# Four layers of long convolutions and a Haar mixing on one core: where the inverse transform's columns, the sums into z and the level steps run

## The chip, the core and the metric

The kernel runs on one core of a Trainium2 chip. A core has a matrix engine (TensorE, in the profile PE, with its weight loads as PEld), VectorE (DVE), ScalarE (ACT), GpSimd (POOL) and SyncE (SP), which here only issues transfers. PE writes its results into PSUM; DVE and ACT read PSUM and the on-chip memory SBUF; GpSimd reads and writes SBUF alone. Each engine works through its own instructions in order and waits for other engines by semaphores. The metric is the device time of one execution in microseconds (us), as the median over runs.

## The reference

The input x has 4 batches of 64 channels of 256 x 256 fp32 values. Four layers follow each other. Layers 0, 1 and 3 are convolutions whose filter is an outer product of two one-dimensional filters, plus a bias term; layer 2 is a two-dimensional Haar transform, a mixing of the channels with a soft threshold, the inverse transform and a residual sum.

```python
# layers 0, 1, 3
hx = _implicit_filter(z, Xw1, Xb1, Xw2, Xb2, Xw3, Xb3, Xwo, Xfreq, t, deltas)
hy = _implicit_filter(z, Yw1, Yb1, Yw2, Yb2, Yw3, Yb3, Ywo, Yfreq, t, deltas)
k = jnp.einsum('ijk,imk->ijmk', hx, hy)[0]
...
y = jnp.fft.irfft2(u_f * k_f, s=(fft_size, fft_size))[..., :L, :L]
out = y + x * bias[:, None, None]

# layer 2
f1 = haar2d(x)
for i in range(v.shape[0]):          # two paths
    f3 = f1 * v[i]
    f4 = jnp.einsum('bchw,oc->bohw', f3, conv_w[i])
    f5 = jnp.sign(f4) * jax.nn.relu(jnp.abs(f4) - tau[i])
    acc = acc + f5
y = haar2d(acc, inverse=True)
return y + x
```

## The kernel before, in words

A separable convolution of one channel is two products with triangular Toeplitz matrices (`contract`, L257 to L262): `first` makes pa, which ACT copies to a (L275), and `second` makes py, to which DVE adds the input times the bias (L292). That DVE step reads py from PSUM and one operand from SBUF. For layer 0 its result is called y0, for layer 1 y1, for layer 3 y3. `pairs` (L337, L338) begins the forward Haar transform along the row on DVE, `levels` goes on with it: lengths 128 and 64 on DVE, the five smaller ones in ten small steps on GpSimd for four channels at a time (L350, L351). `split`, `rest` and `down` turn the columns by two PE matmuls with an fp32r matrix of signs (pz, L381), and `away` sends the coefficients to memory.

`mixing` then takes the coefficients in 64 groups g a batch. `mix` multiplies with the channel weights into a PSUM tile px (L449); `scaled` on DVE (L468) and `scaled_too` on ACT (L473, one instruction of 64 columns each) multiply by v and leave f4. Of 16 parts of a group, N_ACT go to ACT. `size` (ACT, L477) writes the magnitude into the tile mag, of which there are two buffers; `sign` (ACT, L480) follows in place; `shrink` (DVE, L484) takes tau off, `signed` (DVE, L488) clamps at zero and multiplies by the sign, both with two SBUF operands; `add` (L494) sums the two paths into two rows of z, in two steps of 256 columns. The next size on the same mag buffer, two groups later, waits for that add. z holds a whole batch: four chunks of 16 channels.

`inverse` takes the 64 channels of z out. `fetch` (ACT, L534) copies one channel, `rows` (L541, L542) transposes and transforms along one axis on PE into a PSUM tile pw. The other axis is done in two ways. For chunk 0 (c < 16), `halves` splits pw into two fp32r parts (an ACT cast L548 and a DVE subtraction L549) and `cols` multiplies each with a matrix of signs on PE into pu (L555). For chunks 1 to 3 the transform is done ahead in z by DVE: `level` runs `halve` (a subtraction L299 and a scalar_tensor_tensor L300) for n = 1, 2, 4 up to 64 row pairs. The largest levels are cut into pieces of 16 row pairs, 1024 columns. `join` (L563, then L566 and L567) adds the kept residual r to pw or pu and interleaves the result into u. Then layer 3 follows, except for every third channel of batches 0 to 2, which `aside` stores and `convolution` takes up again during mixing 3, in place of the next batch's convolutions.

The order of the work: each stage is put into a list of events by `at`, with a time in ticks from the table PLACE; the list is sorted and recorded in that order. A scheduler then orders each engine's instructions by this order and by what is ready, so a step whose inputs are ready can be moved ahead of others. `tc.add_manual_dep` draws an edge between two instructions that keeps their order on the engine without a semaphore. While mixing b runs, batch b + 1 goes through layers 0 and 1 (`spread`), and inverse b follows the mixing.

Of the kernel before, what the change touches and what calls it, by code (L numbers as in the profile page):

```python
# [12 lines left out]
ALU = mybir.AluOpType  # L13
# [3 lines left out]
B, C, S, EMB, ORD = 4, 64, 256, 33, 64  # L17
# [3 lines left out]
GT = 4  # L21
BUFS = {"res": 1, "y": 5, "co": 3}

N_ACT = (12, 12, 12, 8)

PLACE = {
    "load": 0.714,
    "a0": 1.643,
    "a0 copy": 1.643,
    "y0": 2.571,  # L30
    "y0 sum": 2.571,
    "a1": 3.5,
    "a1 copy": 3.5,
    "y1": 4.429,
# [63 lines left out]
def conv_seq_kernel(ctx, tc, x, fz, fw, bias, decay, haar, haar_row, factors, vt, taut, wmix, out):  # L98
# [14 lines left out]
    nc = tc.nc  # L113
# [19 lines left out]
    bsb = const.tile([P, 3, C], F32, name="bsb")  # L133


    z = zpool.tile([P, 4, P, 4, 16], F32, name="z")
# [118 lines left out]
    def bank(name):  # L255
        return psm.tile([P, 2, S], F32, name=name, tag="mm")

    def contract(ps, src, t):

        for m in range(2):  # L260
            nc.tensor.matmul(ps[:, m, :], src[:, 0, m * P : (m + 1) * P], t[:, ::-1], start=True, stop=False)  # L261
            nc.tensor.matmul(ps[:, m, P:], src[:, 1, m * P : (m + 1) * P], t[:, : P - 1 : -1], start=False, stop=True)  # L262
# [16 lines left out]
    def second(b, st, key, layer, res, new, tag, ahead=None):  # L279


        def product(c):
            s = st[c]
            if ahead is not None:
                s[ahead] = toeplitz(ahead, c, f"t{ahead}_{b}_{c}")
            s["p" + new] = bank(f"p{new}_{b}_{c}")
            contract(s["p" + new], s[key], s[layer][:, 1, :])

        def residual(c):
            s = st[c]  # L290
            y = io.tile([P, 2, S], F32, name=f"{new}_{b}_{c}", tag=tag, bufs=BUFS[tag])
            nc.vector.scalar_tensor_tensor(y, s[res], bsb[:, layer, c : c + 1], s["p" + new], ALU.mult, ALU.add)  # L292
            s[new] = y

        return [product, residual]

    def halve(even, odd):

        nc.vector.tensor_sub(odd, even, odd)  # L299
        nc.vector.scalar_tensor_tensor(even, even, 2.0, odd, ALU.mult, ALU.subtract)  # L300

    def level(n, chunk, begin=0, count=None):
# [3 lines left out]
        halve(v[:, begin : begin + count, 0, 0, :], v[:, begin : begin + count, 1, 0, :])  # L306

    def butterfly():

# [9 lines left out]
    def at(time, run, unit):  # L319
        events.append((time, len(events), run, unit))  # L320
# [104 lines left out]
    def mixing(b, start, n_act):  # L425

        st = {}

        def load(g):
            f = mx.tile([P, 2, S], F32, name=f"f_{b}_{g}", tag="f", bufs=3)  # L430
            nc.sync.dma_start(f, coef[b].rearrange("k c p w -> (k c) p w")[:, 2 * g : 2 * g + 2])
            st[g] = {"f": f}
            if g % GT == 0:
                t = mx.tile([P, 2, GT, 16], F32, name=f"vt_{b}_{g}", tag="vt")
                nc.sync.dma_start(t, scales[g // GT])
                st["vt", g // GT] = t

        def scale(g, i):
            return st["vt", g // GT][:, i, g % GT, :]

        def over(g, i, n):
            return scale(g, i)[:, :n].unsqueeze(2).to_broadcast([P, n, C])

        def mix(g):
            f = st[g]["f"]
            ps = psx.tile([P, 2, 2, S], F32, name=f"px_{b}_{g}", tag="mix")
            for q in range(2):
                for h in range(2):
                    nc.tensor.matmul(  # L449
                        ps[:, q, h, :],  # L450
                        f[:, q, h * P : (h + 1) * P],
                        wb.rearrange("p r n -> p (r n)"),
                        start=True,
                        stop=True,
                    )
            if g == 0:

                one, two = ps[:, 0, :, :P], ps[:, 0, :, P:]
                d = mx.tile([P, 2, P], F32, name=f"d_{b}", tag="mag")
                nc.vector.tensor_copy(d, two)  # L460
                nc.vector.tensor_sub(two, one, d)
                nc.vector.tensor_add(one, one, d)
            st[g]["f4"] = mx.tile([P, 16, C], F32, name=f"f4_{b}_{g}", tag="f4")
            st[g]["px"] = ps.rearrange("p q h (r i o) -> p (q h r i) o", r=2, i=2)

        def scaled(g):
            px, n = st[g]["px"], 16 - n_act
            nc.vector.tensor_tensor(st[g]["f4"][:, :n], px[:, :n], over(g, 0, n), ALU.mult)  # L468

        def scaled_too(g, half):  # L470
            px, f4 = st[g]["px"], st[g]["f4"]
            for j in range(16 - n_act + half * (n_act // 2), 16 - (1 - half) * (n_act - n_act // 2)):
                nc.scalar.mul(f4[:, j], px[:, j], scale(g, 0)[:, j : j + 1])  # L473
# [12 lines left out]
        def signed(g):  # L486
            mag = st[g]["mag"]
            nc.vector.scalar_tensor_tensor(mag, mag, 0.0, st[g]["f4"], ALU.max, ALU.mult)  # L488

        def add(g):  # L490
            parts = st.pop(g)["mag"].rearrange("p (q x i) (n c) -> p q i x n c", q=2, i=2, n=4)
            for q in range(2):
                to = slot(2 * g + q)
                nc.vector.tensor_add(  # L494
                    z[:, :, to].rearrange("p n x c -> p x n c"), parts[:, q, 0], parts[:, q, 1]
                )


        for g in range(S // 4):
            for name, stage in zip(  # L500
                ("mix load", "mix", "scaled", "scaled too", "scaled rest", "size", "sign", "shrink", "signed", "add"),
                (
                    load,
                    mix,
                    scaled,
                    lambda g: scaled_too(g, 0),
                    lambda g: scaled_too(g, 1),
                    size,
                    sign,
                    shrink,  # L510
                    signed,
                    add,
                ),
            ):
                at(start + g + PLACE[name if b + 1 < B else "l " + name], stage, g)

    def inverse(b, start, put_off):

        st = {}

        def early(c):
            tag, bufs = ("f", 3) if c < 20 or c % 5 < 3 else ("f4", 2)
            r = mx.tile([P, 2, 2, P], F32, name=f"r_{b}_{c}", tag=tag, bufs=bufs)
            nc.sync.dma_start(r, keep[b][c])
            st[c]["r"] = r
# [34 lines left out]
        def join(c):  # L560
            ps = st[c]["pw"]
            t = io.tile([P, 2, 2, P], F32, name=f"t_{b}_{c}", tag="res", bufs=BUFS["res"])
            nc.vector.scalar_tensor_tensor(t, st[c]["r"], 0.5, ps, ALU.mult, ALU.add)  # L563
            u = io.tile([P, 2, S], F32, name=f"u_{b}_{c}", tag="y", bufs=BUFS["y"])
            v = u.rearrange("p m (w e) -> p m w e", e=2)
            nc.vector.tensor_add(v[:, :, :, 0], t[:, 0], t[:, 1])  # L566
            nc.vector.tensor_sub(v[:, :, :, 1], t[:, 0], t[:, 1])  # L567
            st[c]["u"] = u
# [3 lines left out]

        along = start - groups - 3

        def when(tick, n, chunk, *span):
            at(tick + PLACE["level"], lambda _: level(n, chunk, *span), 0)
# [88 lines left out]
    ahead = C  # L665
# [128 lines left out]
```

## Time and profile before

| what | us |
|---|---|
| median of 3 runs (2875.58 to 2878.57) | 2876.38 |
| the profiled execution | 2874.07 |
| its span in the trace | 2872.3 |
| ACT: a copies L275, 768 | 478.8 |
| ACT: scaled parts L473, 2816 | 610.5 |
| DVE: shrink L484 and signed L488, 256 each | 316.6 each |
| DVE: residual sums y0 and y1, L292, 256 each | 190.9 and 190.7 |
| DVE: levels of 1024 columns, L299 and L300, 84 each | 102.6 and 103.0 |
| POOL: all | 334.4 |

The profile shows each engine's busy time, and, for a group of instructions, the count, the summed time, the mean of one in ns, and the idle time of the engine ahead of it with what ended that idle time. Times in the trace count from the start of the span. The records of neighbouring instructions on an engine overlap a little, since an instruction is recorded from its start to its last write, so a sum of records can be larger than the time that the engine gave to them.

The batches' mixings lie, by the px matmuls, at 455 to 854, 1072 to 1507, 1720 to 2156 and 2366 to 2637 us; one group takes 6.28, 6.89, 6.89 and 4.31 us in them. The inverses, by the zc copies, lie at 868 to 1062, 1522 to 1711, 2171 to 2361 and 2650 to 2868.

### The profile page before, as it was taken

Reading aid. Unit: us, or ns where it says so; the run is one execution under the profiler, and the core shown is the slowest. Engines: PE = TensorE matmul, PEld = TensorE weight load, DVE = VectorE, ACT = ScalarE, POOL = GpSimd, SP = SyncE. Lnnn points to the kernel's source line nnn. Section 1 sums busy time; section 2 is a strip of 40 time slices with the busy share of each in tenths; the row PEclk is TensorE's granted clock in tenths of the full one; section 3 lists DMA queues with packets and bytes.
Section 4 is the critical chain, followed back from the end, with each engine's and each line's share of the span. In section 5 each row is a group of like instructions: output and inputs, shape, how many; then the busy total and the mean of one; then the engine's idle time right before and its main releaser. Section 6 shows DMA issues by size and latency. Waiting matters only on the chain. (4 is left out here: it accounts for less than half of the span.)

```text
span 2872.3 us, 52434 instructions
## 1 busy us (share of the span) xinstructions
PE 2827.1 (98%) x16592; PEld 2555.6 (89%) x16592; DVE 2494.9 (87%) x4255; ACT 2080.3 (72%) x4950; POOL 334.4 (12%) x644
## 2 busy tenths in 40 slices
PE   9999999999999999999999999999999999999999
PEld 7899998898888898998898998998898998888998
DVE  4655558999999779999999779999999779999985
ACT  2333338999995558998985658999995659998554
POOL 0111111121121001221221001121121000000000
PEclk9999999999999999999999999999999999999999
DMA  6878787776667986777777986777777988787786
GB/s 182 249 231 230 232 232 227 207 208 204 205 209 213 289 254 198 214 213 214 209 207 236 299 255 196 213 214 216 208 208 235 297 266 235 229 238 212 224 241 201
DMA packets 599367, 649.77 MB, mean 226 GB/s; under 512 B 48465, under 2 KB 517044, under 8 KB 598964
## 3 DMA queue, kind: packets, MB, share of 16 engines
q1 hardware_dynamic: 536996, 578.61, 68.9%
q10 hardware_dynamic: 62096, 67.82, 6.7%
q8 instruction: 134, 2.20, 0.3%
q14 instruction: 141, 1.16, 0.1%
HBM read 426.77 MB, written 219.48 MB: 225 GB/s over the span
## 5 line engine op out<-in xcount | busy, mean ns | idle before, releaser
L261 PE MATMUL py<-t,a 128*128 128x256 f32 x3072 | 922.5, 382 | 9.5 <-ACT a L275 8.7
L275 ACT COPY a<-pa 128x512 f32<-128x512 f32 x768 | 478.8, 623 | 498.6 <-PE pa L262 455.2
L473 ACT ACTIVATE f<-px,vt 128x64 f32<-128x64 f32 x2816 | 610.5, 367 | 101.6 <-DVE f L468 101.1
L262 PEld LDWEIGHTS py<-t,a 128*128 128x128 f32 x3072 | 583.4, 190 | 79.3
L262 PE MATMUL py<-t,a 128*128 128x128 f32 x3072 | 590.0, 274 | 0.0
L261 PEld LDWEIGHTS py<-t,a 128*128 128x128 f32 x3072 | 497.3, 191 | 51.2 <-ACT a L275 19.0
L449 PE MATMUL px<-wb,f 128*128 128x256 f32 x2048 | 487.6, 380 | 7.6 <-ACT f L473 7.6
L449 PEld LDWEIGHTS px<-wb,f 128*128 128x128 f32 x2048 | 369.0, 190 | 50.0 <-ACT f L473 10.5
L351 POOL TENSOR_TENSOR sd<-less 128x128 f32<-128x128 f32 (+4 forms) x320 | 190.8, 596 | 1858.7 <-DVE less L350 1519.9
L534 ACT COPY zc<-z 128x512 f32<-128x512 f32 x256 | 282.1, 1105 | 108.1 <-PE pw L542 99.0
L484 DVE TENSOR_TENSOR mag<-mag,vt 128x1024 f32<-128x1024 f32 x256 | 316.6, 1237 | 12.3 <-ACT mag L477 11.5
L488 DVE SCALAR_TENSOR_TENSOR mag<-mag,f 128x1024 f32<-128x1024 f32 x256 | 316.6, 1238 | 0.0
L261 PE MATMUL pa<-t,y 128*128 128x256 f32 x1024 | 309.1, 384 | 6.8 <-DVE y L292 5.2
L261 PE MATMUL pa<-t,x 128*128 128x256 f32 x1024 | 305.9, 381 | 0.5 <-DMA t<-pad 0.5
L477 ACT ACTIVATE mag<-f 128x1024 f32<-128x1024 f32 x256 | 295.7, 1155 | 2.8 <-DVE z L494 0.4
L374 DVE TENSOR_TENSOR sp<-sd,sp 128x512 fp32r<-128x512 f32 x256 | 179.8, 702 | 129.3 <-ACT sp L369 128.2
L480 ACT ACTIVATE f<-f 128x1024 f32<-128x1024 f32 x256 | 285.8, 1116 | 3.5
L261 PE MATMUL pa<-t,u 128*128 128x256 f32 x772 | 233.2, 384 | 6.5 <-ACT w L548 2.8
L292 DVE SCALAR_TENSOR_TENSOR y<-x,bsb,py 128x512 f32<-128x512 f32 x256 | 190.9, 746 | 41.9 <-PE py L262 41.0
L262 PEld LDWEIGHTS pa<-t,x 128*128 128x128 f32 x1024 | 194.6, 190 | 26.3
L262 PEld LDWEIGHTS pa<-t,y 128*128 128x128 f32 x1024 | 194.5, 190 | 26.3
L292 DVE SCALAR_TENSOR_TENSOR y<-y,bsb,py 128x512 f32<-128x512 f32 x256 | 190.7, 745 | 26.0 <-PE py L262 25.6
(73 smaller groups left out, 4412.3 us busy)
## 6 DMA issues: line engine op xcount, KB each, us to landing
t<-pad SPq DMA_DIRECT2D x768, 256.0 KB, 4.1
x<-in_x SPq DMA_DIRECT2D x256, 256.0 KB, 3.7
coef<-co SPq DMA_DIRECT2D x256, 256.0 KB, 3.2
f<-coef SPq DMA_DIRECT2D x256, 256.0 KB, 3.2
r<-keep SPq DMA_DIRECT2D x256, 256.0 KB, 4.1
out_y<-y ACTq DMA_DIRECT2D x193, 256.0 KB, 4.3
keep<-sums SPq DMA_DIRECT2D x256, 128.0 KB, 2.8
keep<-sd SPq DMA_DIRECT2D x256, 128.0 KB, 2.8
```

Of the source, the lines that this page charges most:

```text
L261: nc.tensor.matmul(ps[:, m, :], src[:, 0, m * P : (m + 1) * P], t[:, ::-1], start=True, stop=False)
L262: nc.tensor.matmul(ps[:, m, P:], src[:, 1, m * P : (m + 1) * P], t[:, : P - 1 : -1], start=False, stop=True)
L275: nc.scalar.copy(a, s["p" + new])
L292: nc.vector.scalar_tensor_tensor(y, s[res], bsb[:, layer, c : c + 1], s["p" + new], ALU.mult, ALU.add)
L351: engine.tensor_tensor(t[:, :, :, half:length], v[..., 0], v[..., 1], ALU.subtract)
L449: nc.tensor.matmul(ps[:, q, h, :], f[:, q, h * P : (h + 1) * P], wb.rearrange("p r n -> p (r n)"), start=True, stop=True,)
L473: nc.scalar.mul(f4[:, j], px[:, j], scale(g, 0)[:, j : j + 1])
L477: nc.scalar.activation(mag, st[g]["f4"], AF.Abs)
L480: nc.scalar.activation(st[g]["f4"], st[g]["f4"], AF.Sign)
L484: nc.vector.tensor_sub(mag, mag, over(g, 1, 16))
L488: nc.vector.scalar_tensor_tensor(mag, mag, 0.0, st[g]["f4"], ALU.max, ALU.mult)
L534: nc.scalar.copy(a.rearrange("p h k i -> p (h k) i"), z[:, c // 16, :, :, c % 16].rearrange("p i x -> p x i"))
```

## The change

For batches 0 to 2 `halves` and `cols` are no longer made: the levels now run over all four chunks of z, and join reads pw directly. Their times are new: during the mixing the levels of up to 16 row pairs of all chunks, those of 32 of chunks 0 and 1, all of 64 of chunk 0 and half of it for chunk 1; during the inverse the rest, in pieces of 8 row pairs (512 columns). The last batch keeps its columns on PE for chunk 0 and its times.

Each piece of a level is tied behind the newest y0 sum or join at the time when it is recorded (`behind`), and so is each signed step of mixings 0 to 2. That is an order on DVE and adds no semaphore.

The sums into z of all groups but the last two of each mixing run on GpSimd.

In mixing 3, ACT takes 6 of 16 scaled parts instead of 8, and DVE 10. The residual tiles r of channels 4 to 19 of batches 0 to 2 may use the buffers f4, which the parts of `halves` had used before.

```diff
-N_ACT = (12, 12, 12, 8)
+N_ACT = (12, 12, 12, 6)
...
+    behind = [None]
...
-            nc.vector.scalar_tensor_tensor(y, s[res], bsb[:, layer, c : c + 1], s["p" + new], ALU.mult, ALU.add)
+            done = nc.vector.scalar_tensor_tensor(y, s[res], bsb[:, layer, c : c + 1], s["p" + new], ALU.mult, ALU.add)
+            if new == "y0":
+                behind[0] = done
...
-    def halve(even, odd):
-
-        nc.vector.tensor_sub(odd, even, odd)
+    def halve(even, odd, stay=False):
+
+        first = nc.vector.tensor_sub(odd, even, odd)
+        if stay and behind[0] is not None:
+            tc.add_manual_dep(first.ins, behind[0].ins.name, order, reason="not ahead of the joins")
...
-            nc.vector.scalar_tensor_tensor(mag, mag, 0.0, st[g]["f4"], ALU.max, ALU.mult)
+            step = nc.vector.scalar_tensor_tensor(mag, mag, 0.0, st[g]["f4"], ALU.max, ALU.mult)
+            if b + 1 < B and behind[0] is not None:
+                tc.add_manual_dep(step.ins, behind[0].ins.name, order, reason="the residual sum goes first")
...
-                nc.vector.tensor_add(
-                    z[:, :, to].rearrange("p n x c -> p x n c"), parts[:, q, 0], parts[:, q, 1]
-                )
+                engine = nc.gpsimd if g + 2 < S // 4 else nc.vector
+                engine.tensor_add(z[:, :, to].rearrange("p n x c -> p x n c"), parts[:, q, 0], parts[:, q, 1])
...
-            tag, bufs = ("f", 3) if c < 20 or c % 5 < 3 else ("f4", 2)
+            tag, bufs = ("f", 3) if c < (4 if b + 1 < B else 20) or c % 5 < 3 else ("f4", 2)
...
-            nc.vector.scalar_tensor_tensor(t, st[c]["r"], 0.5, ps, ALU.mult, ALU.add)
+            behind[0] = nc.vector.scalar_tensor_tensor(t, st[c]["r"], 0.5, ps, ALU.mult, ALU.add)
...
-        for chunk in range(1, 4):
-            turn = start + 16 * (chunk - 1)
-            for n in (1, 2, 4, 8):
-                when(along + 12 + 3 * chunk if b + 1 < B else turn, n, chunk)
-            when(turn + 1, 16, chunk)
-            for i in range(2):
-                when(turn + 2 + 2 * i, 32, chunk, 16 * i, 16)
+        if b + 1 < B:
+            for chunk in range(4):
+                for n in (1, 2, 4, 8):
+                    when(along + 12 + 3 * chunk, n, chunk)
+                when(along + 20 + 3 * chunk, 16, chunk)
+            for chunk in range(2):
+                for i in range(2):
+                    when(along + 37 + i + 3 * chunk, 32, chunk, 16 * i, 16)
+                for i in range(3 - chunk):
+                    when(along + 43 + 8 * i + 3 * chunk, 64, chunk, 16 * i, 16)
+            when(along + 63, 64, 0, 48, 8)
+            when(start - 0.2, 64, 0, 56, 8)
             for i in range(4):
-                when(turn + 6 + 2 * i, 64, chunk, 16 * i, 16)
+                piece(start + 4 + 2 * i, 64, 1, 32 + 8 * i, 8)
+            for chunk in range(2, 4):
+                turn = start + 20 * chunk - 32
+                for i in range(4):
+                    piece(turn + i, 32, chunk, 8 * i, 8)
+                for i in range(8):
+                    piece(turn + 4 + 2 * i, 64, chunk, 8 * i, 8)
+        else:
...
-            if c < 16:
+            if c < 16 and b + 1 == B:
```

In the `else` the last batch's levels stand with the times that they had; `when` and `piece` both pass `stay=True`.

More of the change, by code (lines that the diff above doesn't have):

```diff
@@ L291, in residual, with level @@
             y = io.tile([P, 2, S], F32, name=f"{new}_{b}_{c}", tag=tag, bufs=BUFS[tag])
-            nc.vector.scalar_tensor_tensor(y, s[res], bsb[:, layer, c : c + 1], s["p" + new], ALU.mult, ALU.add)
+            done = nc.vector.scalar_tensor_tensor(y, s[res], bsb[:, layer, c : c + 1], s["p" + new], ALU.mult, ALU.add)
+            if new == "y0":
+                behind[0] = done
             s[new] = y
         return [product, residual]
-    def halve(even, odd):
-        nc.vector.tensor_sub(odd, even, odd)
+    def halve(even, odd, stay=False):
+        first = nc.vector.tensor_sub(odd, even, odd)
+        if stay and behind[0] is not None:
+            tc.add_manual_dep(first.ins, behind[0].ins.name, order, reason="not ahead of the joins")
         nc.vector.scalar_tensor_tensor(even, even, 2.0, odd, ALU.mult, ALU.subtract)
-    def level(n, chunk, begin=0, count=None):
+    def level(n, chunk, begin=0, count=None, stay=False):
         count = n if count is None else count
         v = z.rearrange("p n s x c -> p n s (x c)")[:, chunk].rearrange("p (j e s) x -> p j e s x", e=2, s=P // 2 // n)
-        halve(v[:, begin : begin + count, 0, 0, :], v[:, begin : begin + count, 1, 0, :])
+        halve(v[:, begin : begin + count, 0, 0, :], v[:, begin : begin + count, 1, 0, :], stay)
     def butterfly():
@@ L573, in inverse, with when, piece @@
         along = start - groups - 3
-        def when(tick, n, chunk, *span):
-            at(tick + PLACE["level"], lambda _: level(n, chunk, *span), 0)
+        def when(tick, n, chunk, begin=0, count=None):
+            at(tick + PLACE["level"], lambda _: level(n, chunk, begin, count, stay=True), 0)
+        def piece(tick, n, chunk, begin, count):
+            at(tick + PLACE["level"], lambda _: level(n, chunk, begin, count, stay=True), 0)
         at(along + 11 + PLACE["level"], lambda _: butterfly(), 0)
-        for chunk in range(1, 4):
-            turn = start + 16 * (chunk - 1)
-            for n in (1, 2, 4, 8):
-                when(along + 12 + 3 * chunk if b + 1 < B else turn, n, chunk)
-            when(turn + 1, 16, chunk)
-            for i in range(2):
-                when(turn + 2 + 2 * i, 32, chunk, 16 * i, 16)
-            for i in range(4):
-                when(turn + 6 + 2 * i, 64, chunk, 16 * i, 16)
+        if b + 1 < B:
[10 more added lines that the diff above has]
+            when(start - 0.2, 64, 0, 56, 8)
+            for i in range(4):
+                piece(start + 4 + 2 * i, 64, 1, 32 + 8 * i, 8)
[6 more added lines that the diff above has]
+        else:
+            for chunk in range(1, 4):
+                turn = start + 16 * (chunk - 1)
+                for n in (1, 2, 4, 8):
+                    when(turn, n, chunk)
+                when(turn + 1, 16, chunk)
+                for i in range(2):
+                    when(turn + 2 + 2 * i, 32, chunk, 16 * i, 16)
+                for i in range(4):
+                    when(turn + 6 + 2 * i, 64, chunk, 16 * i, 16)
         for c in range(C):
```

## The prediction

> **What bounds the kernel now.** I read four views, in this order: the busy times of the page, a table of windows cut at the stages (a mixing begins with its first px and ends where the first zc of its inverse starts, within some microseconds), the groups of instructions with shapes kept apart, and the timeline of PE, DVE and POOL in three short stretches.
>
> ```profile
> PE 2827.1 (98%) x16592; PEld 2555.6 (89%) x16592; DVE 2494.9 (87%) x4255; ACT 2080.3 (72%) x4950; POOL 334.4 (12%) x644
> ```
>
> ```profile
> core 0: us, PE busy (x) PEld busy (x) DVE busy (x) ACT busy (x) POOL busy (x), PEclk, DMA share, GB/s
> 440.00:857.00 417.00, 411.31 (x2278) 367.00 (x2277) 406.85 (x684) 386.26 (x1104) 81.85 (x130) 1.00 0.70 209
> 857.00:1052.00 195.00, 186.87 (x1202) 170.17 (x1201) 167.24 (x301) 114.89 (x150) 10.01 (x20) 0.99 0.84 257
> 1052.00:1500.00 448.00, 445.79 (x2510) 401.78 (x2509) 431.72 (x719) 392.51 (x1111) 88.03 (x140) 1.00 0.71 209
> 1500.00:1698.00 198.00, 195.76 (x1269) 179.51 (x1268) 164.83 (x306) 121.99 (x165) 7.60 (x20) 1.00 0.86 269
> 2345.00:2630.00 285.00, 277.32 (x1516) 248.21 (x1515) 277.61 (x411) 265.80 (x694) 0.00 (x0) 1.00 0.79 233
> ```
>
> The rows are mixing 0, inverse 0, mixing 1, inverse 1 and mixing 3; mixing 2 and inverse 2 repeat 1. PE is idle for 5.7, 8.1, 2.2, 2.2 and 7.7 us in them: it sets the pace everywhere, and only three stages have something to win back. In the mixings DVE is a second bound, 96 to 98% busy.
>
> ```profile
> L494 DVE TENSOR_TENSOR z<-mag 128x256 f32<-128x256 f32 x512 | 204.4, 437 | 0.5
> L555 PE MATMUL pu<-w,hb 128*128 128x512 f32 x128 | 46.5, 439 | 0.0
> L549 DVE TENSOR_TENSOR w<-pw,w 128x512 fp32r<-128x512 f32 x64 | 43.6, 686 | 0.2 <-ACT w L548 0.2
> L351 POOL TENSOR_TENSOR sd<-less 128x128 f32<-128x128 f32 x64 | 84.0, 1312 | 1858.7 <-DVE less L350 1519.9 <-ACT f L473 155.6 <-ACT a L275 66.1
> ```
>
> Records overlap, so an instruction's price on a full engine is the step from its start to the next start. Timelines:
>
> ```profile
> 1544.61 0.71 PE L555 MATMUL pu<-w,hb 128*128 128x512 f32 x2
> 1545.15 0.59 PE L261 MATMUL py<-t,a 128*128 128x256 f32 x2
> ...
> 804.94 0.45 DVE L338 TENSOR_TENSOR sd<-y 128x256 f32<-128x256 f32 x1
> 805.27 0.72 DVE L374 TENSOR_TENSOR sp<-sd,sp 128x512 fp32r<-128x512 f32 x1
> 805.88 1.25 DVE L488 SCALAR_TENSOR_TENSOR mag<-mag,f 128x1024 f32<-128x1024 f32 x1
> 807.01 0.78 DVE L292 SCALAR_TENSOR_TENSOR y<-x,bsb,py 128x512 f32<-128x512 f32 x1
> ```
>
> ```profile
> 101.24 0.45 POOL L351 TENSOR_TENSOR sd<-less 128x128 f32<-128x128 f32 x1 [19.65 <-DVE less L350]
> 102.37 0.29 POOL L351 TENSOR_TENSOR sd<-less 128x64 f32<-128x64 f32 x1
> ```
>
> ```profile
> 804.80 2.96 POOL L350 TENSOR_TENSOR less<-less 128x128 f32<-128x128 f32 x2 [0.53 <-DVE sd L351]
> 807.97 4.93 POOL L350 TENSOR_TENSOR less<-less 128x32 f32<-128x32 f32 x1
> ```
>
> A pu pair costs PE 0.54 us. DVE steps are 0.33 us for 256 columns, 0.61 for 512, 1.13 for 1024. A GpSimd operation of 128 columns takes 0.45 us when DVE leaves it alone; at 804.80 two of them took 2.96, and one of 32 columns took 4.93 instead of about 0.24. It moves only beside DVE steps that read PSUM (the residual at 807.01); beside DVE steps with two SBUF inputs it stands.
>
> **The change, part by part.**
>
> *Columns of three batches leave PE.* 3 x 16 pairs at 0.54 us: **-25.9 us** on the engine that sets the end. The low bound is 22.6 (0.47 a pair: at 1548.10 a transpose and the pair together take 0.58, and the transpose alone 0.11). ACT loses 48 casts of 0.59 us (L548) and DVE 48 subtractions, 48 x 0.61 = 29 us; both sit beside PE work, so nothing further is counted. r's buffers change for channels 4 to 19; number and size of the DMAs stay, so zero. If a transfer came late, join would wait, as it does now for 9.9 us in ten places (L563 on r).
>
> *The levels on DVE.* By the recorded order, mixings 1 and 2 hold 70 level steps each before, 56 us at the prices above, and 66 after, 42 us; mixing 0 has 41 and then 42; mixing 3 14 and then 5; inverses 1 and 2 none and then 34 us each; inverse 0 15 and then 34; inverse 3 41 and then 50. Batch 0 to 2's chunk 0 adds 20 us a batch, and cutting pieces to 512 columns costs 2 x 0.61 against 1.13.
>
> *The sums into z.* 496 steps x 0.33 = 166 us leave DVE, 41 a mixing, against an own record mean of 437 ns. On GpSimd 256 columns are not in the trace: from 0.29 at 64 and 0.45 at 128 the line gives 0.77; by the shortest records (0.287 and 0.402) it gives 0.63; the mean of the 128-column rows in place, 1.31, is the upper end for one that waits. I take 0.7: 62 x 2 x 0.7 = 87 us of work in a mixing.
>
> *Together, mixing 1:* DVE 432 - 41 - 14 = 377 of 448 us. To it comes what GpSimd holds up. The longest DVE record beside a 128-column GpSimd operation is 0.24 us over its median; scaled by 0.7/0.45 this is 0.37 an add, 124 x 0.37 = 46 us at most, and nothing at least. So DVE ends between 377 and 423, below PE's 446. GpSimd needs 87 plus 14 sets of level steps at some 2.6 us (their length at 101.24), 123 us; DVE's PSUM-reading steps (y0, y1, scaled) offer about 1.5 us in each 6.9 us group, 96 us, and its idle 25 to 70 us more. It fits, closely.
>
> *The skill against this.* The Trainium skill, "SBUF — State Buffer", section "Who interferes with whom", says the port pair shared by VectorE and GpSimd is an exclusive lock, and that a VectorE instruction with two SBUF inputs and a GpSimd one that reads SBUF block each other fully. The 4.93 us row agrees for GpSimd; for DVE this trace shows a smaller toll. "GPSIMD Engine Reference", section 3.1, measures a GpSimd add at 1.96 times VectorE's; an estimate from that is 0.86 us beside the 437 ns row, and if each add blocked DVE for all of it, mixing 1 would hold 377 + 107 = 484 us of DVE and grow by 36. I hold to the rows.
>
> *The tie of the signed step.* DVE is in order: a signed step now waits, with all behind it, for the newest y0, thus for py on PE. Behind it come the add, then the mag buffer (two of them), then size of group g+2 on ACT, and behind that the a copies PE needs. From the ends of L488 and the starts of L477 two groups later, the median room is 6.7 us in mixing 0, 8.0 in 1 and 2, and 3.4 in 3. Two adds, each in a window of its own, take some 3 to 4 us. I price this at +2 us a mixing for the first three (bounds 0 and the rival below), **+6**.
>
> *Inverses 1 and 2* gain 34 us of levels and lose 10 (16 subtractions): DVE 165 - 12 - 10 + 34 = 177 in 198 - 9 = 189 us, 94%. I add 2 us each, **+4** (bounds 0 and 8). *The junctions:* fetch of channel 0 now needs the last level piece, two steps of 0.61 behind the last add. PE has the next batch's tail meanwhile, so at most 3 x 1.2; I take **+2**.
>
> *Won back:* mixing 3's DVE goes from 278 to 278 - 41 - 9 + 64 x 0.13 (two more scaled columns) = 236, and ACT loses 128 of L473 at 0.2 us, 266 to 240. PE is left to set it; of its 7.7 us idle I take 5. Inverse 0 loses the subtractions in its full first part: 6 of 8.1. Mixing 0: 2 of 5.7. Sum **-13**.
>
> Total: -25.9 + 6 + 4 + 2 - 13 = -27 on the profiled execution's 2874.07 us (span 2872.3 and 1.8 around it), 2847. The median of the runs is 2.3 above that execution, so **2849**.
>
> **Rivals.** *A, more is won back:* all 21.5 us of idle in the three stages, none of the 12 added: 2876 - 26 - 21 = 2829. For it: DVE gets 55 us of air in mixing 1. Against: PE waits there too for ACT (8.7 us in py on L275), which is little eased before mixing 3.
>
> *B, GpSimd falls behind: slower.* Once in four channels its set of ten level steps goes ahead of the adds: in the mixing 803.87 to 813.76, 9.9 us, elsewhere 6 to 7. Adds behind it end 10 to 11 us after their signed step, past the room of 8.0, and ACT stands with the a copies behind it. There are 48 sets; ACT has 448 - 393 = 55 us of idle a mixing to absorb them. From 0.6 us of PE wait per set on, the 26 us are gone; at 1 us it is 2876 - 26 + 48 = 2898. Against it: the room was measured with DVE full.
>
> *C, nothing:* the stalls just eat the PE work (0.5 us a set): 2876. *That the change does not do what it says* is excluded: 32 pu matmuls stand in the new program where 128 did.
>
> **How the numbers follow.** The forecast has 0.58 (own range 2834 to 2866), A 0.14, C 0.10, B 0.18. The range takes in A, C and the near part of B: 2824 to 2884. What can be told from no change is 0.2%, 5.8 us; from the cases: faster 0.72, within 0.09, slower 0.19.
>
> **What would show it.** In the new profile: pu matmuls x32; mixing 1 still about 446 us of PE in 448 with DVE near 400; z sums on POOL with means of 1.0 to 2.0 us. Wrong, if ACT's size waits long for POOL's z (B), if DVE stays at 96% or more in the mixings, if inverses 1 and 2 take over 195 us, or if PE waits for y.

## The result and the profile after

The changed kernel takes 2947.84 us (median of 4 runs, 2945.93 to 2950.95) against 2876.46 for the kernel before (4 runs): 1.0253 times as long, 95% interval 1.0240 to 1.0265. The forecast was 2849, in 2824 to 2884. The profiled execution has a span of 2944.1 us, 71.8 more than before.

From the page of the changed kernel, the busy line, three rows of the 40 slices and three groups (summed time, mean ns of one, idle time ahead and what ended it):

```profile
PE 2841.9 (97%) x16496; PEld 2535.9 (86%) x16496; DVE 2467.3 (84%) x3867; ACT 2032.5 (69%) x4774; POOL 736.8 (25%) x1140
...
DVE  4665557999888978999898977999898988998996
ACT  2333348898885557888885557888885558888544
POOL 0111113353430003344340003334341003442000
...
L503 POOL TENSOR_TENSOR z<-mag 128x256 f32<-128x256 f32 x496 | 450.1, 928 | 1288.0 <-DVE mag L494 962.5
...
L490 DVE TENSOR_TENSOR mag<-mag,vt 128x1024 f32<-128x1024 f32 x256 | 333.8, 1304 | 68.3 <-ACT mag L483 67.3
...
L380 DVE TENSOR_TENSOR sp<-sd,sp 128x512 fp32r<-128x512 f32 x256 | 196.9, 769 | 153.0 <-ACT sp L375 152.6
```

PE has 96 matmuls fewer and still more busy time. A record of 256 columns lasts 0.38 us while the next matmul starts after 0.22, so wherever the next one comes late more of a record counts as busy. VectorE gave up 388 instructions, and its busy time fell by only 28 us. The same subtraction L374 that took 702 ns a piece before takes 769 as L380, shrink 1304 instead of 1237. GpSimd works in all four mixings, and most of its idle time ahead of the sums (962.5 of 1288.0 us) is spent waiting for VectorE.

The table of windows: mixing 0, inverse 0, mixing 1, inverse 1, mixing 3. A mixing is cut from its first px to the first zc, an inverse from there to its last zc. The places of the stages in "Time and profile before" lie 11.1 us later than in this count from the start of the span (mixing 0 begins at 443.9 in it); their lengths hold.

```profile
core 0: us, PE busy (x) PEld busy (x) DVE busy (x) ACT busy (x) POOL busy (x), PEclk, DMA share, GB/s
446.00:898.00 452.00, 425.35 (x2307) 370.77 (x2307) 405.90 (x585) 389.79 (x1107) 183.92 (x255) 1.00 0.66 196
898.00:1077.00 179.00, 171.23 (x1113) 154.49 (x1112) 158.51 (x307) 102.36 (x127) 6.64 (x20) 1.00 0.85 266
1087.00:1563.00 476.00, 461.22 (x2553) 408.89 (x2552) 428.02 (x614) 400.38 (x1124) 185.80 (x264) 1.00 0.68 201
1563.00:1748.00 185.00, 177.75 (x1146) 160.12 (x1145) 163.81 (x317) 105.42 (x132) 7.04 (x20) 1.00 0.86 266
2424.00:2710.00 286.00, 274.84 (x1482) 241.66 (x1480) 259.24 (x277) 243.49 (x574) 106.70 (x124) 1.00 0.77 228
```

By the same marks (first px to last px, on to the first zc, on to the last zc) the kernel before has 399.0, 435.2, 435.1 and 271.5 us in the mixings, and the changed one 425.9, 454.0, 453.5 and 274.5: +67. The stretches from a mixing's last px to the inverse's first zc grow by 23 in all, the gaps before a mixing by 5, and the inverses shrink by 24. Mixing 1 from its first px to its last, before (first row) and after:

```profile
1060.50:1495.60 435.10, 432.88 (x2429) 389.84 (x2428) 423.15 (x705) 386.31 (x1093) 84.38 (x132) 1.00 0.71 207
1086.80:1540.80 454.00, 439.65 (x2429) 389.90 (x2429) 409.02 (x585) 384.43 (x1083) 181.87 (x261) 1.00 0.67 199
```

So the mixings are longer, with VectorE at 90% in mixing 1 where it was at 97%, and PE has 14.4 us of idle time there where it had 2.2. The engine that sets the end waits, and no engine is as full as PE was before (432.88 of 435.10 us).

Who makes it wait, from the view of the waits (total us, times, longest):

```profile
DVE y L294 <- PE py L264: 158.4, 176, 6.9
...
DVE mag L490 <- ACT mag L483: 67.3, 76, 2.6
PEld py L263 <- ACT a L277: 47.2, 93, 2.0
...
PE px L455 <- ACT f L479: 24.2, 34, 1.6
PE py L263 <- ACT a L277: 20.6, 37, 1.8
...
ACT mag L483 <- POOL z L503: 7.8, 9, 1.2
...
PE pa L263 <- DVE y L294: 4.7, 7, 1.6
```

Before, the first five were 122.0, 11.5, 19.0, 7.6 and 8.7 us, the wait for POOL had no counterpart, and PE waited 5.2 us for y. The engines wait for each other in a circle, VectorE for PE and ACT, PE for ACT. Nearly nobody waits for the sum itself: the row with POOL, the mechanism of rival B, is 7.8 us in all. What the sums do is seen in the timeline of mixing 1:

```profile
1134.31 1.42 POOL L503 TENSOR_TENSOR z<-mag 128x256 f32<-128x256 f32 x2 [7.39 <-DVE mag L494]
...
1135.14 0.87 DVE L343 TENSOR_TENSOR sums<-y 128x256 f32<-128x256 f32 x1
...
1135.93 0.41 DVE L344 TENSOR_TENSOR sd<-y 128x256 f32<-128x256 f32 x1
...
1137.56 1.22 DVE L494 SCALAR_TENSOR_TENSOR mag<-mag,f 128x1024 f32<-128x1024 f32 x1
...
1138.86 2.41 POOL L503 TENSOR_TENSOR z<-mag 128x256 f32<-128x256 f32 x2 [3.13 <-DVE mag L494]
...
1139.00 1.67 DVE L490 TENSOR_TENSOR mag<-mag,vt 128x1024 f32<-128x1024 f32 x1 [0.23 <-ACT mag L483]
```

L343 runs beside the tail of two GpSimd sums and takes 0.87 us; L344, of the same size, follows when they are done and takes 0.41. L490, with a median of 1.22, takes 1.67, and the two sums beside it take 2.41 where the pair above took 1.42. Each engine holds the other.

I sum this over the trace as "hold": for each VectorE record that overlaps a GpSimd record, its length less the median of its line and size. The kernel before has 9.9 us of hold, the changed one 88.1: 22, 27, 27 and 10 in the four mixings. The longest single hold is 0.60 us.

### The profile page after: what moved, and what is told of

The parts are those of the page before. It is cut to its first block, busy times and chain, and to the rows that moved or that the text cites. A ratio compares the mean times of both kernels' runs of the same rounds, so it can differ in the third digit from the quotient of the medians.

```text
span 2944.1 us, 52325 instructions
## 1 busy us (share of the span) xinstructions
PE 2841.9 (97%) x16496; PEld 2535.9 (86%) x16496; DVE 2467.3 (84%) x3867; ACT 2032.5 (69%) x4774; POOL 736.8 (25%) x1140
## 5 line engine op out<-in xcount | busy, mean ns | idle before, releaser
L263 PE MATMUL py<-t,a 128*128 128x256 f32 x3072 | 927.6, 384 | 21.2 <-ACT a L277 20.6
L503 POOL TENSOR_TENSOR z<-mag 128x256 f32<-128x256 f32 x496 | 450.1, 928 | 1288.0 <-DVE mag L494 962.5
L479 ACT ACTIVATE f<-px,vt 128x64 f32<-128x64 f32 x2688 | 591.7, 365 | 127.0 <-DVE f L474 125.8
L455 PE MATMUL px<-wb,f 128*128 128x256 f32 x2048 | 499.4, 382 | 24.4 <-ACT f L479 24.2
L490 DVE TENSOR_TENSOR mag<-mag,vt 128x1024 f32<-128x1024 f32 x256 | 333.8, 1304 | 68.3 <-ACT mag L483 67.3
L380 DVE TENSOR_TENSOR sp<-sd,sp 128x512 fp32r<-128x512 f32 x256 | 196.9, 769 | 153.0 <-ACT sp L375 152.6
L357 POOL TENSOR_TENSOR sd<-less 128x128 f32<-128x128 f32 (+4 forms) x320 | 132.9, 415 | 608.3 <-DVE less L356 551.0
```

What stands on the lines that cost most here:

```text
L380: nc.vector.tensor_tensor(w[:, 1], t, w[:, 0].bitcast(F32), ALU.subtract)
L455: nc.tensor.matmul(ps[:, q, h, :], f[:, q, h * P : (h + 1) * P], wb.rearrange("p r n -> p (r n)"), start=True, stop=True,)
L503: engine.tensor_add(z[:, :, to].rearrange("p n x c -> p x n c"), parts[:, q, 0], parts[:, q, 1])
```

## The experiments

Sixteen kernels, in four groups. In the first table "sums" says where the sums into z of groups 0 to 61 are made; the runs of the kernel before, taken beside them, had medians of 2876.7 to 2877.5.

| kernel | columns of batches 0 to 2 | sums | levels' tie | signed tie | us | ratio to before, 95% interval |
|---|---|---|---|---|---|---|
| before | PE | VectorE | no | no | 2877 | |
| a_cols_only | VectorE | VectorE | no | no | 2877.5 | 0.9992 to 1.0015 |
| a_tie_only | VectorE | VectorE | no | yes | 2885.0 | 1.0017 to 1.0040 |
| a_stay_only | VectorE | VectorE | yes | no | 2915.1 | 1.0110 to 1.0173 |
| a_adds_dve | VectorE | VectorE | yes | yes | 2942.1 | 1.0181 to 1.0267 |
| a_free | VectorE | GpSimd | no | no | 2972.5 | 1.0311 to 1.0371 |
| a_no_stay | VectorE | GpSimd | no | yes | 2956.7 | 1.0241 to 1.0309 |
| a_no_tie | VectorE | GpSimd | yes | no | 2936.2 | 1.0174 to 1.0233 |
| after | VectorE | GpSimd | yes | yes | 2947.8 | 1.0240 to 1.0265 |
| a_cols_pe | PE | GpSimd | yes | yes | 2977.8 | 1.0324 to 1.0384 |
| b_adds_pool | PE | GpSimd | no | no | 2962.2 | 1.0264 to 1.0324 |

| kernel | what | us | ratio to before, 95% interval |
|---|---|---|---|
| a_no_adds | after, without the sums of groups 0 to 61 | 2914.2 | 1.0104 to 1.0163 |
| b_no_adds | before, without these sums | 2872.6 | 0.9972 to 0.9994 |
| c_no_adds | a_cols_only, without these sums | 2851.2 | 0.9889 to 0.9930 |
| b_echo | before, and GpSimd reads each finished row of z | 2973.7 | 1.0315 to 1.0375 |
| c_act8 | a_cols_only, ACT keeps 8 parts in mixing 3 | 2874.7 | 0.9987 to 1.0006 |
| c_stay_mix | a_cols_only and the levels' tie in the mixings | 2900.2 | 1.0065 to 1.0095 |
| c_stay_inv | a_cols_only and the levels' tie in the inverses | 2884.8 | 1.0014 to 1.0034 |

### One part of the change undone

My first theory was that VectorE pays for the sums on GpSimd; the rivals were the two ties.

```diff
 a_adds_dve
-                engine = nc.gpsimd if g + 2 < S // 4 else nc.vector
+                engine = nc.vector
 a_no_tie
-            if b + 1 < B and behind[0] is not None:
+            if False:
 a_no_stay
-        if stay and behind[0] is not None:
+        if False:
 b_adds_pool (kernel before)
-                nc.vector.tensor_add(
+                engine = nc.gpsimd if g + 2 < S // 4 else nc.vector
+                engine.tensor_add(
```

> The changed kernel with all sums into z back on VectorE. Theory P (GpSimd's sums hold the port that VectorE's steps with two SBUF inputs need; the records beside GpSimd are 88 us over their medians, 10 before): the mixings shrink by most of the 65 us that they gained, about 2885 us or less. Theory T (the signed step tied behind y0 keeps f4 and px): the time stays at 2940 to 2970, since VectorE gets 166 us more and the tie stays. Theory L (the levels' new times): 2940 or more too.

> The changed kernel with the signed steps of mixings 0 to 2 free. Theory T: PE's waits for px (38 us more in mixings 0 to 2 than before) go, 2895 to 2915 us. Theory P: within 10 us of 2948. Theory L: within 10 us of 2948.

> The changed kernel with the level pieces free, so that the scheduler may pull them into the mixings as it did before. Theory L (levels during the inverses hold the joins, and PE loses 4 to 9 us in 50 there): 2915 to 2930 us. Theories P and T: the mixings get some 13 us of VectorE work each, the same or up to 30 us slower, 2945 to 2980.

> The kernel before with nothing changed but the sums into z, on GpSimd for all groups but the last two of a mixing. Theory P: slower than before by the greater part of 71 us, 2915 to 2940. Theory T or L: faster or the same, 2860 to 2880, since VectorE is rid of 166 us.

Measured: 2942.1, 2936.2, 2956.7 and 2962.2. No single part, undone, brings the time back, and the sums alone, put into the kernel before, cost it 85 us; its mixing 1 grows from 435.2 to 460.2. So there are at least two causes, and each can cover the other. That called for the other corner of the table, the parts one by one.

### The columns alone, and the sums left out

a_cols_only has the columns and the new times of the levels, with the sums on VectorE and neither tie (the first three edits above in one). a_cols_pe is the changed kernel with the columns of PE and the levels' times of the kernel before. a_no_adds and b_no_adds leave out 496 of 512 sums; z is cleared once by GpSimd during the first convolutions. With no sum to wait for, a level step without a tie can also run much earlier than it could in a kernel that makes the sums, so these runs change two things, the load and the place of the levels.

```diff
 a_no_adds (b_no_adds likewise)
-                engine = nc.gpsimd if g + 2 < S // 4 else nc.vector
+                if g + 2 < S // 4:
+                    continue
 a_cols_pe
-            if c < 16 and b + 1 == B:
+            if c < 16:
```

> The changed kernel without the sums into z of groups 0 to 61 of each mixing, on either engine; z is cleared once by GpSimd in the first convolutions. Left out: 496 sums. Theory P (GpSimd's sums, by the port and by their latency, cost the mixings): PE sets the mixings again, 435 us each for 1 and 2, 2860 to 2880 in all. Theory O (the order that the ties, the levels' times and the scheduler give the engines is what costs): the mixings keep 448 to 455 us, 2925 us or more.

> The columns of three batches on VectorE with the new times of the levels, without either tie and with all sums on VectorE. Theory O with the ties to blame: 2880 or less, as a_adds_dve (2942) has both ties beside it. If the columns and levels alone cost the time: 2930 or more.

> Sums on GpSimd and both ties, but the columns on PE and the levels with their times of before: what the columns add is the difference to 2948. If the columns are worth their 26 us of PE work: 2965 to 2980. If what they add to VectorE costs more than that: 2900 to 2935.

> The kernel before without the sums into z of groups 0 to 61 of each mixing; z is cleared once by GpSimd. Left out: 496 sums, 166 us of VectorE. Theory P: 2855 to 2870, the 21 us of PE's idle time come back in part. Theory O (any change of what VectorE holds upsets the order): slower than 2876.

Measured: 2914.2, 2877.5, 2977.8 and 2872.6. Where the level steps ran, as the sum of their records in us (a mixing up to the first zc of its inverse, an inverse up to the next px; c_no_adds follows further on):

| kernel | ahead of mixing 0 | mixing 0 | inverse 0 | mixing 1 | inverse 1 | mixing 3 |
|---|---|---|---|---|---|---|
| before | 0 | 37 | 25 | 52 | 10 | 12 |
| b_no_adds | 54 | 0 | 14 | 47 | 14 | 52 |
| a_cols_only | 0 | 49 | 38 | 57 | 29 | 8 |
| c_no_adds | 81 | 2 | 11 | 75 | 11 | 51 |
| after | 0 | 51 | 38 | 51 | 38 | 7 |
| a_no_adds | 1 | 48 | 39 | 47 | 39 | 6 |

Three readings follow. The ties cost a lot with no sum anywhere (a_no_adds is 37 over the kernel before). The levels stay in their stages in it, so the load of the sums can be read there: with both ties they cost 34 us on GpSimd (2947.8 to 2914.2) and 28 on VectorE (2942.1), a good part of the 28 by a lower granted clock (last section).

The columns alone win nothing, though beside ties and GpSimd they are worth 30 (2977.8 to 2947.8). Part of the reason stands in the stages of a_cols_only: inverses 0 to 2 are 17 us shorter than in the kernel before, but mixing 0, where VectorE is busy 421 of 432 us up to the first zc, has 12 us more level steps and takes 12.5 us longer.

And taking 166 us of sums off VectorE in the kernel before wins 4 us. Mixing 1, where PE is full, goes from 435.2 to 434.0: there the air on VectorE has almost no worth. The 4 us of the whole are a balance, though. From the first px of mixing 0 to that of mixing 3 b_no_adds takes 1893 us where the kernel before takes 1911; the part ahead of it grows by 6, and mixing 3, into which 40 us of level steps have moved, by 11.

### The sums alone, the ties alone, and GpSimd's presence alone

a_free is a_cols_only with the sums on GpSimd; a_tie_only and a_stay_only are a_cols_only with one tie. b_echo leaves all sums of the kernel before on VectorE and lets GpSimd read each finished row into a tile that nobody uses:

```diff
 b_echo (kernel before)
                 nc.vector.tensor_add(
                     z[:, :, to].rearrange("p n x c -> p x n c"), parts[:, q, 0], parts[:, q, 1]
                 )
+                if g + 2 < S // 4:
+                    row = z[:, :, to].rearrange("p n x c -> p x n c")
+                    for h in range(2):
+                        nc.gpsimd.tensor_add(junk, row[:, 2 * h : 2 * h + 2], row[:, 2 * h : 2 * h + 2])
```

> The changed kernel with neither tie: columns on VectorE, sums on GpSimd. Against a_cols_only (2877.5, sums on VectorE) only the sums' engine differs. Theory P (GpSimd's sums cost 26 us a mixing wherever they stand): 2940 to 2965. Theory T (the ties cost, and the sums cost only beside the ties): 2870 to 2890.

> a_cols_only with the tie of the signed step added, level pieces free, sums on VectorE. If the signed step behind y0 is what costs (px frees late): 2915 to 2945, with PE's waits for px near 40 us. If it is the tie of the levels: 2877 to 2885.

> a_cols_only with the tie of the level pieces added, signed steps free, sums on VectorE. If the levels' tie is what costs: 2915 to 2945. If it is the signed step's: 2877 to 2885.

> The kernel before, sums on VectorE, and after each sum two GpSimd additions of 128 columns that read the finished row and write to a tile that nobody reads: GpSimd's load of the change without anyone waiting for its result. Theory P by the port: 2900 to 2945, VectorE's records beside GpSimd 40 us or more over their medians. Theory P by waiting (VectorE's levels and ACT's size stand behind GpSimd's sums): 2876 to 2885.

Measured: 2972.5, 2885.0, 2915.1 and 2973.7. The sums on GpSimd cost 95 us without a tie (2877.5 to 2972.5), and b_echo costs 97 with every sum where it was and with its level steps in the same stages as before. Its groups and waits:

```profile
L501 POOL TENSOR_TENSOR junk<-z 128x128 f32<-128x128 f32 x992 | 698.0, 704 | 1062.2 <-DVE z L495 998.6 <-issue 4.0 <-POOL junk L501 0.4
...
L489 DVE SCALAR_TENSOR_TENSOR mag<-mag,f 128x1024 f32<-128x1024 f32 x256 | 330.7, 1293 | 0.0
```

```profile
PEld pa L262 <- DVE y L293: 77.6, 76, 2.6
PE pa L262 <- DVE y L293: 57.9, 63, 2.4
...
DVE z L300 <- POOL junk L501: 22.6, 21, 2.0
```

The signed step L489 takes 1293 ns where it took 1238, and PE now waits 57.9 us for the residual sums y of VectorE, where it waited 5.2. The hold is 90.2 us. Only the third row is a wait for GpSimd: a level must not overwrite a row that the echo still reads. So GpSimd's presence is enough to cost the kernel before 97 us, up to these 22.6. VectorE is nearly full there (445 of 464 us in mixing 1, which grew by 29), so its hold of 22 us there falls on an engine with little room. The run doesn't show that hold costs as much where VectorE was relieved, as in the changed kernel, and it can't part the hold from the order in which VectorE's steps then come.

a_free waits at two more places, which the ties close:

```profile
PE pa L263 <- DVE y L294: 69.9, 65, 2.3
...
DVE z L303 <- POOL z L503: 49.3, 39, 3.1
ACT mag L483 <- POOL z L503: 46.7, 24, 3.5
```

In a_free a level step whose rows GpSimd has not yet finished stands at the head of VectorE's queue for 49.3 us in all, and size for a mag buffer for 46.7. In the changed kernel these are under 5 and 7.8. The free level steps also crowd into the mixings: 95 us of them in mixing 1 of a_free, 55 in a_no_tie. Both go with the levels' tie, which is dear without GpSimd (+38) and gains 36 with it; the runs don't part the two.

### What the columns lack, and which half of the tie costs

Open was why 26 us less PE work (96 matmuls of 512 columns at 0.27 us from start to start, half of the pair's 0.54) win nothing in a_cols_only, and where the levels' tie costs. c_no_adds leaves the 496 sums out of a_cols_only as above; the others are small:

```diff
 c_act8 (a_cols_only)
-N_ACT = (12, 12, 12, 6)
+N_ACT = (12, 12, 12, 8)
 c_stay_mix (a_stay_only; c_stay_inv with > for <)
-            at(tick + PLACE["level"], lambda _: level(n, chunk, begin, count, stay=True), 0)
+            at(tick + PLACE["level"], lambda _: level(n, chunk, begin, count, stay=tick < start - 0.1), 0)
```

> Columns of three batches on VectorE, no ties, and without the 496 sums of groups 0 to 61 (they are left out; z is cleared once by GpSimd during the first convolutions). Theory 'no room on VectorE': the columns' 26 us were not won in the kernel with the sums on VectorE (2877.5) because VectorE, at 97% in the mixings, had taken on 512 columns of level steps per piece for them; with 166 us of sums gone there is room, and the time falls to about 2850. Theory 'PE waits elsewhere': PE's nine saved us per batch turn into waits for ACT's and VectorE's copies at the joins and in mixing 0, whose chain is latency and not load; then the sums make no more difference than in the kernel before (-4), and the time is about 2873.

> Columns on VectorE, sums on VectorE, no ties, and ACT keeps 8 of 16 scaled parts in mixing 3, as before. In the profile mixing 3 took 276.0 us with 6 and 271.5 in the kernel before: if that is the price of the two parts moved to VectorE while the sums are there, the time is 2873, 0.1 to 0.2% under the kernel before. If mixing 3 is set by something else, 2877 stays.

> Columns and sums on VectorE, no signed tie; of the levels only the pieces that are due during the mixing are tied behind y0, those due in the inverse are free. Both halves tied gave 2915.1, none 2877.5. Theory 'ties in the mixing': a level step recorded behind y0 may no longer fill the idle time ahead of that y0, and holds it on VectorE instead: most of the 38 us, 2905 or more. Theory 'pieces of the inverse': free, these are pulled into the idle time of the mixing, tied they fill the inverse and the junction: then this run is at 2885 or less.

> The other half: only the pieces due in the inverse are tied (behind joins), those of the mixing are free. Theory 'ties in the mixing': 2885 or less. Theory 'pieces of the inverse': 2905 or more. If both halves come out near 2895 the cost is shared, and if both come out near 2880 it needs both at once.

Measured: 2851.2, 2874.7, 2900.2 and 2884.8. With the sums left out the columns are worth 21 us (2872.6 to 2851.2), with the sums in place nothing; and leaving the sums out is worth 26 beside the columns (2877.5 to 2851.2) and 4 without. So each gains by the other. The windows show where the room is missing, the first 28 and the next 40 us of inverse 1, in a_cols_only:

```profile
1520.60:1548.60 28.00, 27.37 (x170) 24.79 (x169) 28.00 (x53) 13.89 (x21) 8.86 (x10) 1.00 0.78 230
1548.60:1588.60 40.00, 36.71 (x231) 31.96 (x230) 39.31 (x78) 20.06 (x26) 3.82 (x10) 1.00 0.81 249
```

and in c_no_adds:

```profile
1504.40:1532.40 28.00, 28.00 (x175) 25.73 (x174) 22.31 (x41) 15.25 (x24) 2.87 (x10) 1.00 0.83 242
1532.40:1572.40 40.00, 38.69 (x254) 34.96 (x253) 31.47 (x63) 22.60 (x28) 3.49 (x10) 1.00 0.91 279
```

In the first, VectorE (third pair) is full to 28.00 of 28 and 39.31 of 40 us, and PE gets 170 and 231 matmuls through; in the second it has 22.31 and 31.47, and PE gets 175 and 254. Over the whole of inverse 1 a_cols_only's VectorE shows 86%, which says nothing of this. The other place is mixing 0, where VectorE is busy 421 of 432 us in a_cols_only and 343 of 412 in c_no_adds. In mixings 1 and 2 the two agree within 0.4 us (434.9 and 435.3).

The room in c_no_adds has a second source, the place of the levels in the table above. In these 68 us level steps take 26 us in a_cols_only and 4 in c_no_adds, more than the whole difference of VectorE (67 and 54 us); and batch 0's steps ran ahead of mixing 0, where no kernel that makes the sums could have them. So the run shows that the columns' PE work can be won where VectorE isn't full, and not what freed time alone would bring.

c_act8 is not apart from the kernel before (its interval holds 1): no kernel of this study that does the whole work beats it. The tie's cost lies mostly in the mixings: +22.7 with the pieces there tied, +7.3 with those of the inverses, +37.6 with both. In the waits of a_cols_only and a_stay_only (first and second fence) it shows as time that VectorE leaves empty:

```profile
DVE sp L380 <- ACT sp L375: 128.0, 86, 2.5
DVE y L294 <- PE py L264: 113.4, 148, 7.0
```

```profile
DVE sp L380 <- ACT sp L375: 141.6, 102, 2.3
DVE y L294 <- PE py L264: 129.9, 150, 6.8
```

VectorE has the same work in both, and with the tie it stands 30 us longer before sp and y. That fits a reading that no run tests by itself: a level step that may run early fills such a wait; one that is tied behind the y0 it should have filled the time before runs after it, when PE wants the next thing.

## Why the prediction was wrong

**"-25.9 us on the engine that sets the end."** PE's work did fall by that, and the inverses of the changed kernel are 24 us shorter. That this shortens the whole was read from PE's small idle times, and failed: a_cols_only is at +1. VectorE bounds mixing 0 and the beginning of an inverse as tightly as PE does. The step took VectorE's share over an inverse (177 in 189 us, 94%) and priced the overload at 4 us; the first 68 us of inverse 1 in a_cols_only, where channels are fetched, joined and levelled at once, are where VectorE is full.

**"DVE ends between 377 and 423, below PE's 446."** As a busy time this was nearly right: 428 us in mixing 1, with 27 us of hold, inside the 0 to 46 that was bounded. (The 14 us by which the level steps were to shrink in the mixing did not come: 52 us before, 51 after.) The inference from it failed: that below PE's time GpSimd's work costs nothing. The price was 0, and the runs show 95 us without ties (a_free) and 85 in the kernel before. The likely way is this: a hold falls on the step that runs, half a microsecond at a time, and all steps behind it in VectorE's queue come later, y for PE's next product, f for the px products, sp for the turn; PE had 2 us of slack in the mixing. It fits PE's waits for y in a_free (69.9 us, 5.2 before), but no run parts it from the changed order of the steps. And it isn't needed for the mixings of the changed kernel: with both ties and the sums on VectorE mixing 1 takes 454.9 us too (a_adds_dve, some 7 of them by half clock), with a hold of 2.5.

**"Won back, -13."** Freed time on VectorE was counted as won in mixings 0 and 3 and in inverse 0. Inverse 0 did shrink by 14.9 us, as much as the columns and this term promised it together; mixing 3 grew by 3 where 5 were to be won, and mixing 0 grew by 27 where 2 were to be won.

**The ties: "+6" and nothing for the levels' tie.** The signed tie alone is +7.5, as priced. The levels' tie had no term of its own and costs 37.6; its steps were costed as work that fits, and that the scheduler had used them as filler for waits was not looked at. Both together are +64.6 with the sums on VectorE, though in a_adds_dve some 22 us of the profiled execution were lost to the granted clock (below), so that sum is less sure.

**The sum.** From before to after by single steps: columns +1, sums to GpSimd +95, levels' tie -36, signed tie +12. In another order: columns +1, levels' tie +38, signed tie +27, sums to GpSimd +6. Both end at +71 to +72, and neither gives a part a price of its own: the same tie is +38 beside VectorE's sums and -36 beside GpSimd's. That c_no_adds lies at 2851, beside the forecast of 2849, is a coincidence: it has the columns moved and the sums gone at no cost, as the forecast described, but also level steps where no kernel that makes the sums could have them.

**Rival B** had the right sign and the wrong way. It let ACT's size wait for the sums and asked for 1 us at 48 places; the wait is 7.8 us. Its argument that GpSimd fits only closely was not what decided: GpSimd was busy 186 of 476 us in mixing 1. Rivals A and C, faster and no change, fell with the step that they share with the forecast, that the columns shorten the time. **The duration of a sum** was right: 0.7 us estimated, 0.733 as the median and 0.928 as the mean. None of the four signs of being wrong came true: size waited 7.8 us for the sums, VectorE fell to 90% in the mixings, inverses 1 and 2 took 185 and 184 us, and PE waited 4.7 us for y where it had waited 5.2. They watched single engines, while the loss came as PE's waits for f, a and sp: 24.2, 20.6 and 12.3 us. Those for f are nearly the same with the sums on VectorE (19.7 in a_adds_dve); those for a are not (5.1).

**The skill's rule** was set aside with the words "for DVE this trace shows a smaller toll", read from operations of 128 columns and fewer, with 0.24 us as the longest hold. Beside sums of 256 columns the longest is 0.60. The Trainium skill, "SBUF — State Buffer", section "Who interferes with whom", has the contention of a VectorE instruction with two SBUF inputs and a GpSimd one that reads SBUF, and calls the pair an exclusive lock; L343 and L490 above agree with that, though a hold of 0.60 us at most is less than a whole sum (0.73). An estimate from its rule and the 1.96 of "GPSIMD Engine Reference", section 3.1, gave 36 us more for mixing 1, where it grew by 19 (26 with the stretch up to the first zc). It was nearer than the price of zero, but partly by luck, since the mixing grew by 20 in a_adds_dve too, without the sums on GpSimd.

**What stays open** is how the 71 us of the changed kernel divide between the hold, the ties and the place of the levels: each of the two causes is shown by runs, their way through the queues is argued.

## What to carry to other kernels

Where two engines are both over nine tenths busy, relief of one can be worth little, and work moved from one to the other nothing: take the sum over short windows, not over stages. Test relief by leaving the work out, and then look where the steps went that had waited for its result, since their move can be a good part of what the run shows. An in-order engine's delays need not be paid from its idle time; ask for each held instruction who waits for the next ones in its queue. And small steps without an urgent reader may be worth something as filler; a tie that keeps them in their place takes that away.

## What the runs showed of the hardware

A GpSimd sum of 256 columns beside two-input VectorE steps costs both engines: 496 of them bring 75 to 97 us of hold on VectorE in the six kernels that have them, while the kernels without GpSimd's sums or reads stay at 6 to 12. 992 reads of 128 columns bring 90, with 0.23 us as the longest hold.

The granted clock of PE falls to 0.5 for 3.4 us or a multiple of it, mostly 2.3 to 4.5 us after the start of a gap between PE's matmuls (a gap is counted from the end of the last matmul's usual step). The kernel before has two such stretches in its record, one of them at its very end. a_adds_dve has eleven, nine of them behind gaps of 2.1 to 3.4 us; PE is busy for 44 us in them, which at half speed is an estimate of 22 us lost. Over all eighteen traces, after 450 us, 8 of 247 gaps of 1.2 to 2.0 us were followed by one, and 31 of 65 gaps of 2.0 to 3.0 us. In a_cols_only PE waits 13.1 us for the first zc of inverse 3, from 2639.0 to 2652.0 us; the clock is at 0.5 from 2642.0 to 2655.7, so only the last 3.6 us of it fall on work. The same pair appears in a_tie_only, a_stay_only, a_adds_dve and the two kernels with half of the tie. The Trainium skill, "TensorE: Matmul & The Clock Gate", Part 1, gives the half rate after an idle window of about 3.4 us; here gaps of little over 2 us went ahead of it about every second time. The changed kernel has only two stretches of about 3 us, so its 72 us are not clock.
